# Graph network, two layers in fp32: stores and sums on GpSimd moved, a normalisation's sums given to ScalarE, the last block's weighted sums by quarters

## Chip, cores and metric

The kernel runs on one core of a Trainium2 chip. The metric is the device time of one execution in microseconds. TensorE is called PE in the profile's lines, VectorE DVE, ScalarE ACT, GpSimd POOL and SyncE SP.

## What is computed

128 graphs of 64 nodes with 768 features pass through two residual layers, each followed by a layer normalisation. All is fp32. The reference, cut to what matters:

```
def layer0(h, adjacency):
    u = einsum('bld,bmd->blm', h, h) / sqrt(d)
    delta = softmax(u) * adjacency
    attn = delta / (sum(delta, axis=2, keepdims=True) + 1e-10)
    h_left, h_self, h_right = h @ W_left.T + b_left, h @ W_self.T + b_self, h @ W_right.T + b_right
    ctx = upper(attn) @ h_left + diagonal(attn) * h_self + lower(attn) @ h_right
    o = (ctx - mean(ctx)) / sqrt(var(ctx) + 1e-12) * gamma + beta
    return relu(o)

def layer1(x, adj):                       # 12 heads of 64
    q, k, v = heads(x @ Wq + bq), heads(x @ Wk + bk), heads(x @ Wv + bv)
    s = q @ k.T / sqrt(64) + beta * adj
    s = where(adj > 0, s, -9e15)
    return merge(softmax(s) @ v)

x = layernorm(x + layer0(x, adj))         # eps 1e-5
x = layernorm(x + layer1(x, adj))
```

## The kernel before

The 8192 node rows are worked in 16 blocks (n = 0 to 15) of 512 tokens: four tiles (T = 4) of 128 tokens, two graphs in each. The large products (left, right, self, values, queries and keys) are not done as plain matrix products. `seven` (L343) does a product as seven sub-products of half size (Strassen-Winograd), each for j = 0 and 1. The sums of inputs that this needs are formed on GpSimd: `combined` (L296 to L301) and `combined4` (L307), tiles `S`. For blocks 3 to 15 (`DEEP` = 3) the left and right products together go through a second level, `nested` (L398) called by `both_sides`, with 49 sub-products of matmuls of 128x384; its inputs `q` are quarter sums from GpSimd (L314 to L317), its weights `wlr` come from DRAM (`lr_d`), where `deepened` put differences of weights (L250) during blocks 0 and 1.

A sub-product accumulates in a PSUM bank, X or Y. Between the sub-products that share a bank the partial result is taken out: in `nested` as `u_deep` or `lr` (L414 by ScalarE where nothing is added, L416 by VectorE), in the self and value products as `u`, `o` and `v` (L393, L567, L718, L723), in the query and key products as `uqk` (L748, ScalarE), `q` and `k` (L754 ScalarE, L756 VectorE). The next sub-product of that bank waits for it.

The loop over n (L961 on) emits, for m = n + 1 and p = n - 1: the left and right products of block m, its self product, the values of block n with the first layer's context of block m between them (`context0`, four parts), then queries and keys of block n in three head groups hg = 0, 1, 2 (`projected`). The second layer's small work is put between the sub-products. For each head group there are `scores` (64 small products, then on VectorE two multiplications L782, add L803, maximum L804, subtract L805; on ScalarE 16 exponentials L796; on VectorE two transpositions L800 of the exponentials, `turn`) and `weighted` (64 small products `ps_y` L824, then on VectorE a reciprocal L830 and four multiply-adds L834 for each of four parts). `finish_by_act` normalises the finished block on ScalarE (sums L865, squares L868, root L870, output L862) and stores it from GpSimd (L863). In block n's `context0` the first normalisation takes its statistics on VectorE (`moments`: bn_stats L331, aggregate L332, root on ScalarE L339), then gamma and beta, relu and residual (L654, L657, L660), the second normalisation's moments, and `norm` (L666), which also stores the tile to DRAM as `x1d` from GpSimd (L668). `x1d` is loaded again in transposing order by ScalarE's DMA queue (`squares`, L275) as `sq`.

The order of all instructions on an engine is the order in which the program emits them. Work on VectorE and ScalarE is held in two lists, `urgent` and `lazy`; after each sub-product `step` hands out one item of them (items marked "act" also leave room for one more). `settle(key)` empties a list up to the named work. The dictionaries left, right, own, val and qk[0..2] hang work on a place: in `seven`, place 2k + j is before half j of the k-th sub-product; in `nested`, the 28 places of left (0 to 13) and right (14 to 27) are spread over the 49 sub-products. The places that matter here, all in the loop: scores(p, 2) at left 1, weighted(p, 1) at left 5, weighted(p, 2) at left 13, finish_by_act(p) at right 0, the loads of `sq` from x1d (`begin1`) at left 10 to 13, combined4 of block m at left 0, weighted(n, 0) at qk[2] 5. Behind the last block, the weighted sums come in six halves of 32 products, each followed by its additions, and `finish` twice.

Of the kernel before, what the change touches and what calls it, by code (L numbers as in the profile page):

```python
# [17 lines left out]
P = 128  # L18
# [5 lines left out]
T = 4  # L24
# [27 lines left out]
def gnn_two_layers(ctx: ExitStack, tc, x, adj, wl, bl, ws, bs, wr, br, gamma, beta,  # L52
# [81 lines left out]
    def step(act_free=True, light=False):  # L134
        for queue in (urgent, lazy):
            if not queue:
                continue
            kind = queue[0][2] if len(queue[0]) > 2 else None
            if light and (queue is lazy or kind is None):
                return  # L140
            if kind == "act" and not act_free:
                continue
            queue.popleft()[1]()
            if kind is None or light:
                return
# [252 lines left out]
    def nested(width, sums, load, multiply, view, C, bias0, bias1, hooks):  # L398
# [65 lines left out]
        for k, i in enumerate(ORDER2):  # L464
            after = ORDER2[k + 1] if k + 1 < len(ORDER2) else None
            if after:
                F[after], W[after] = sums(after), load(after)
            for j in (6, 5, 7):
                sub(i, j)
            if after:  # L470
                sub(after, 1)
                sub(after, 2)
            for j in (4, 3):
                sub(i, j)
# [159 lines left out]
    def context0(n):  # L634

        blk = blocks[n]
        xa, o, dg = blk["xa"], blk["x"], blk["dg"]

        def part(t):
# [8 lines left out]
            if t == T - 1:  # L648
                rest()

        key = ("o", n)

        def affine(t, mean, rstd):
            nc.vector.scalar_tensor_tensor(o[t], o[t], mean, affine_of["gamma"], ALU.subtract, ALU.mult)  # L654
# [10 lines left out]
        def norm(t, mean, rstd):  # L665
            nc.vector.tensor_scalar(o[t], o[t], mean, rstd, ALU.subtract, ALU.mult)  # L666
            if squared:
                nc.gpsimd.dma_start(out=x_d[t * P : (t + 1) * P, :], in_=o[t])  # L668

        def rest():  # L670
            for t, mr in enumerate(moments(key, o, 1e-12)):
                later(key, partial(affine, t, *mr), partial(affine2, t, *mr), partial(residual, t))
            for t, mr in enumerate(moments(key, o, 1e-5)):
                later(key, partial(norm, t, *mr))

        return [partial(part, t) for t in range(T)]
# [28 lines left out]
    def values(n, hooks={}, in_place=False):  # L705
# [8 lines left out]
        def last(t, h, ps, part):  # L714
            add = pairs(bias["v"][:, h * HALF : (h + 1) * HALF] if part is None else part)
            heads = slice(h * 3, (h + 1) * 3)
            if not in_place:
                nc.vector.tensor_tensor(v[:, t, :, heads, 0:HD], pairs(ps), add, ALU.add)  # L718
                return
            for r in range(2):  # L720
                for g in range(2):
                    rows = slice(g * L, (g + 1) * L)
                    nc.vector.tensor_tensor(v[r * L : (r + 1) * L, t, g, heads, 0:HD],  # L723
                                            pairs(ps)[rows, r], add[rows, r], ALU.add)

        by_tokens("v", blocks[n]["S"], last, None, hooks)
        if not in_place:
            low, high = v[0:L, :, 1, :, 0:HD], v[L:P, :, 0, :, 0:HD]
            swap = l0t.tile([P, T, HP, HD], F32, tag="lr", name="swap")
            later(("v", n), act(lambda: nc.scalar.copy(swap[0:L], high)), act(lambda: nc.scalar.copy(high, low)),  # L730
                  act(lambda: nc.scalar.copy(low, swap[0:L])), queue=urgent)
# [77 lines left out]
    def weighted(n, hg, halves=range(2)):  # L809
# [7 lines left out]
        for h in halves:  # L817
            for t in range(2):
                for c in range(2):
# [7 lines left out]
        def added(h, r):  # L827
            ps = y[r, h]
            rz = st.tile([P, 2, 2], F32, tag="rz1", name="rz1")
            nc.vector.reciprocal(rz, ps[:, :, :, HD])  # L830
            for t in range(2):
                res = xt[2 * h + t].rearrange("p (c k r d) -> p r c k d", c=2, k=HC, r=2)
                for c in range(2):
                    nc.vector.scalar_tensor_tensor(res[:, r, c, hg, :], ps[:, t, c, 0:HD], rz[:, t, c : c + 1],  # L834
# [5 lines left out]
    def finish_by_act(n):  # L840
# [19 lines left out]
        def norm(ts):  # L860
            for t in ts:
                nc.scalar.activation(xt[t], xt[t], AF.Identity, bias=shift[:, t : t + 1], scale=rstd[:, t : t + 1])  # L862
                nc.gpsimd.dma_start(out=out_t[n, t], in_=xt[t])  # L863
# [7 lines left out]
              act(partial(norm, (0, 1))), act(partial(norm, (2, 3))), queue=urgent)  # L871
# [42 lines left out]
    now(context0(0))  # L914
# [35 lines left out]
    for n in range(NBLK):  # L950
# [12 lines left out]
        for i, (when, hooks, place) in zip(ORDER2, ((0, val, 2), (0, val, 8), (0, qk[0], 8), (0, qk[1], 6),  # L963
                                                    (0, qk[2], 6), (1, left, 2), (1, right, 4))):
# [6 lines left out]
        if p >= 0:  # L971
            one, two, three = (left, left, right) if not last else (qk[0], qk[1], qk[1])
            at(one, 1 if not last else 2, scores, p, 2, 1 if last else 2)
            at(one, 5, weighted, p, 1)
            at(two, 13 if not last else 5, weighted, p, 2)
            at(three, 0 if not last else 6, finish if last else finish_by_act, p)

        if not last:
            if n > 0:
# [9 lines left out]
                at(left, 10, begin1)  # L989
# [8 lines left out]
                for a in range(P // Q):  # L998
                    at(left, 10 + a, lambda a=a: sq1["fs"][a]())
# [14 lines left out]
                at(left, 0, lambda: combined4(blocks[m]["S"]))  # L1014
# [20 lines left out]
            for t, f in enumerate(context0(m)):  # L1035
                at(val, 1 + 2 * t, f)
            if m + 1 < NBLK:
# [25 lines left out]
        if not last:  # L1063
            at(qk[2], 5, weighted, n, 0)
        for hg in range(NHG):
            projected(n, hg, qk[hg])
    n = NBLK - 1
    values(n, {6: [partial(scores, n, 2, 2, l0t)]}, True)

    for h in range(2):  # L1070
        for hg in range(NHG):
            weighted(n, hg, (h,))
            settle(("y", n, hg))
        finish(n, range(2 * h, 2 * h + 2))
        settle(("f", n))
# [31 lines left out]
```

## Time and profile before

| | us |
|---|---|
| three runs | 2980.74, 2976.38, 2977.93 |
| median | 2977.93 |
| the profiled execution | 2979.73 |
| its span | 2978.0 |
| PE busy | 2881.8 |
| VectorE busy | 2062.7 |
| ScalarE busy | 994.4 |
| GpSimd busy | 713.0 |
| block 3's stretch, 627 to 807, PE busy | 177.31 of 180.0 |
| the last 110 us, PE busy | 89.95 |

A busy time is the sum of an engine's instructions; weight loads (PEld) run beside the matmuls. The granted clock is the share of its full rate that TensorE was given in a stretch. Idle time is charged by the profile to what seemed to release the engine.

### The profile page before, as it was taken

How to read it: one execution, taken by the hardware profiler on the slowest of the kernel's cores; microseconds unless marked ns; L12 is line 12 of the kernel's file. 1: busy time of each engine (PE TensorE's matmuls, PEld its weight loads, DVE VectorE, ACT ScalarE, POOL GpSimd, SP SyncE). 2: the span in 40 equal slices, each digit the busy share in tenths (PEclk: the TensorE clock that was granted, in tenths of full speed). 3: DMA queues.
4: the chain of work that ended last, by engine and by line, in shares of the span. 5: the costliest groups of instructions: out<-in, count | busy, mean ns of one | idle time of the engine just before them, and what ended most of it. 6: DMA issues, size and time to landing. Idle time of an engine off the chain costs nothing.

```text
span 2978.0 us, 49826 instructions
## 1 busy us (share of the span) xinstructions
PE 2881.8 (97%) x17578; PEld 1940.8 (65%) x17578; DVE 2062.7 (69%) x4219; ACT 994.4 (33%) x1848; POOL 713.0 (24%) x881
## 2 busy tenths in 40 slices
PE   8899899999999999999999999999999999999997
PEld 5557558576675756758566575766758566585685
DVE  5858767677686766757667676776867667577657
ACT  0102305334243351424425253342433514244242
POOL 3133311405023040321304123050230403213010
PEclk9999999999999999999999999999999999999998
DMA  9678875958669495775957759486694957858442
GB/s 328 204 258 271 243 203 158 277 143 257 180 176 265 138 286 156 203 237 155 269 151 219 225 164 274 138 247 191 184 260 136 286 154 191 246 153 273 130 123 86
DMA packets 440149, 613.17 MB, mean 206 GB/s; under 512 B 53584, under 2 KB 416720, under 8 KB 439904
## 3 DMA queue, kind: packets, MB, share of 16 engines
q1 hardware_dynamic: 361808, 492.79, 55.0%
q10 hardware_dynamic: 60848, 44.05, 8.0%
q0 software_dynamic: 17248, 73.15, 6.6%
q8 instruction: 143, 2.34, 0.3%
q14 instruction: 102, 0.84, 0.1%
HBM read 539.43 MB, written 77.27 MB: 207 GB/s over the span
## 4 chain that ended last, share of the span: by engine, by line
PE 79%; DVE 6%; issue 6%; ACT 5%; DMA 3%; POOL 1%; SPq 0%; ACTq 0%; POOLq 0%; DVEq 0%
PE ps_X L362 32%; PE ps_Y L362 24%; PE ps_Y L613 9%; PE ps_X L613 8%; PE ps_ctx L644 3%; ACT eT L796 3%; PE u L504 1%; PE ps_y L824 1%; PE sc L778 1%; DMA wlr<-lr_d 1%; ACT L796 1%; DVE lr L416 1%; DVE mx L804 1%; DVE s L782 1%; DVE s L805 0%
## 5 line engine op out<-in xcount | busy, mean ns | idle before, releaser
L748 ACT ACTIVATE uqk<-ps_X,bq 128x256 f32<-128x256 f32 x144 | 68.2, 473 | 1056.4 <-PE ps_X L362 909.2
L362 PE MATMUL ps_X<-xT,wqk 128*128 128x256 f32 x1728 | 390.8, 380 | 3.5 <-ACT uqk L748 3.4
L362 PEld LDWEIGHTS ps_X<-xT,wqk 128*128 128x128 f32 x1728 | 329.2, 191 | 52.5 <-ACT uqk L748 4.3
L796 ACT ACTIVATE eT<-s 32x256 f32<-32x256 f32 x768 | 317.8, 414 | 36.8 <-DVE s L805 26.6
L296 POOL TENSOR_TENSOR S<-hT 128x768 f32<-128x768 f32 x16 | 28.9, 1808 | 1157.3 <-PE ps_Y L362 1120.3
L362 PE MATMUL ps_Y<-S,wqk 128*128 128x256 f32 x1152 | 264.3, 379 | 0.0
L362 PEld LDWEIGHTS ps_Y<-S,wqk 128*128 128x128 f32 x1152 | 218.9, 190 | 29.8
L613 PE MATMUL ps_Y<-wlr,q 128*128 128x384 f32 x546 | 208.6, 491 | 0.0
L416 DVE TENSOR_TENSOR lr<-ps_Y,u_deep 128x384 f32<-128x384 f32 x273 | 151.5, 555 | 75.1 <-PE ps_Y L613 66.9
L362 PE MATMUL ps_X<-wv,xT 128*128 128x384 f32 x576 | 195.3, 489 | 0.1
L362 PE MATMUL ps_X<-ws,hT 128*128 128x384 f32 x540 | 181.7, 490 | 4.3 <-DVE u L393 3.0
L613 PE MATMUL ps_X<-wlr,q 128*128 128x384 f32 x364 | 150.1, 494 | 23.9 <-POOL q L314 17.0
L834 DVE SCALAR_TENSOR_TENSOR o<-ps_y,rz,o 128x64 f32<-128x64 f32 x768 | 165.1, 278 | 6.8
L362 PEld LDWEIGHTS ps_X<-wv,xT 128*128 128x128 f32 x576 | 108.1, 190 | 81.3 <-issue 9.0
L362 PEld LDWEIGHTS ps_X<-ws,hT 128*128 128x128 f32 x540 | 103.0, 192 | 77.8 <-DVE u L393 3.6
L416 DVE TENSOR_TENSOR u_deep<-ps_X,lr 128x384 f32<-128x384 f32 x195 | 107.8, 553 | 60.4 <-PE ps_X L613 54.7
L756 DVE TENSOR_TENSOR q<-ps_Y,uqk 128x256 f32<-128x256 f32 x144 | 60.3, 419 | 124.3 <-ACT uqk L748 73.1
L613 PEld LDWEIGHTS ps_Y<-wlr,q 128*128 128x128 f32 x546 | 101.6, 190 | 67.2
L393 DVE TENSOR_TENSOR u<-ps_X,bv 128x384 f32<-128x384 f32 x96 | 52.8, 550 | 128.8 <-PE ps_X L362 128.7
L362 PE MATMUL ps_X<-S,wqk 128*128 128x256 f32 x576 | 138.3, 385 | 0.0
L296 POOL TENSOR_TENSOR S<-xT 128x768 f32<-128x768 f32 x16 | 28.9, 1806 | 452.3 <-DVE xT L284 323.8
L362 PE MATMUL ps_Y<-xT,wqk 128*128 128x256 f32 x576 | 135.6, 385 | 0.0
(238 smaller groups left out, 5441.2 us busy)
## 6 DMA issues: line engine op xcount, KB each, us to landing
wlr<-lr_d SPq DMA_DIRECT2D x819, 192.0 KB, 3.7
wqk<-qk_d SPq DMA_DIRECT2D x672, 192.0 KB, 2.4
wv<-d_v SPq DMA_DIRECT2D x192, 192.0 KB, 2.9
ws<-d_s SPq DMA_DIRECT2D x180, 192.0 KB, 5.3
wv<-in_L_gnn_Wv_dram SPq DMA_DIRECT2D x144, 192.0 KB, 4.1
ws<-in_L_gnn_W_self_dram SPq DMA_DIRECT2D x135, 192.0 KB, 5.5
xa<-in_x_dram SPq DMA_DIRECT2D x64, 384.0 KB, 6.4
out_dram<-o POOLq DMA_DIRECT2D x64, 384.0 KB, 6.6
```

The lines of the kernel that those rows point to most:

```text
L296: nc.gpsimd.tensor_tensor(s1, a21, a22, ALU.add)
L362: nc.tensor.matmul(ps, lhsT=a, rhs=b, start=(c == 0 and i in (1, 2, 5)), stop=(c == len(fs) - 1), skip_group_check=True)
L393: nc.vector.tensor_tensor(u, ps, bias[nm][:, b * HALF : (b + 1) * HALF], ALU.add)
L416: nc.vector.tensor_tensor(dst, view(ps), add, ALU.add)
L504: nc.tensor.matmul(u[g * L : (g + 1) * L, t, :], lhsT=xT[:, c, tok], rhs=xT[:, c, tok], start=(c == 0), stop=(c == KC - 1))
L613: nc.tensor.matmul(ps, lhsT=a, rhs=b, start=(k == 0 and j in (1, 2, 5)), stop=(k == len(fs) - 1), skip_group_check=True)
L644: nc.tensor.matmul(ps[g * L : (g + 1) * L, 0:HALF], lhsT=blk["aT"][:, t, g * L : (g + 1) * L], rhs=blk["lr"][t][:, g, cols], start=True, s ...
L748: nc.scalar.activation(u, ps, AF.Identity, bias=bias["qk"[j]][:, c : c + 1])
L756: nc.vector.tensor_tensor(dst, ps, part, ALU.add)
L778: nc.tensor.matmul(sc[r][g * L : (g + 1) * L, t, c, :], lhsT=q[rows, c, tok], rhs=k[rows, c, tok], start=True, stop=True)
L796: nc.scalar.activation(e[cols, :, rows], pairs[rows, :, cols], AF.Exp)
L834: nc.vector.scalar_tensor_tensor(res[:, r, c, hg, :], ps[:, t, c, 0:HD], rz[:, t, c : c + 1], res[:, r, c, hg, :], ALU.mult, ALU.add)
```

## The change

It has nine parts. `step` runs items marked "free" at the head of a list without using up its step. The stores of x1d and of the output are split off from the normalisations as such free items. The last group of a second-level product does sub-product 3 before 4. `context0` of blocks after the first takes its sums on ScalarE: one Identity with accumulation after each part, four squares at val 9 (`squares`), the root at val 13 (`roots`), reciprocal and the rest at qk[0] 1 (`inverse`). In the last block v is written in one operation for each half, ScalarE then exchanges its halves by three copies for each quarter, and the weighted sums run by quarters (a half of the tiles, a half of the heads), seven of twelve between the value products. Two of the weight matrices of `deepened` (i = 4, 3) move from left 2 and right 4 of block 1 to own 3 and val 3. scores(p, 2) moves from left 1 to 2; weighted(p, 2) from left 13 to right 1 and finish_by_act from right 0 to 2 where m >= DEEP. The loads of sq from x1d start at right 2 in block 1 alone. combined4 of block m moves from left 0 to left 6, weighted(n, 0) from qk[2] 5 to 11.

```
@@ step
         for queue in (urgent, lazy):
+            while queue and queue[0][2:] == ("free",):
+                queue.popleft()[1]()
@@ nested
-            for j in (4, 3):
+            for j in (4, 3) if after else (3, 4):
@@ context0
+        by_act = n > 0
...
-            if t == T - 1:
-                rest()
+            if by_act:
+                nc.scalar.activation(unused(), o[t], AF.Identity, accum_out=total[:, t : t + 1])
+            elif t == T - 1:
+                rest(moments(key, o, 1e-12))
+        def squares():
+            nc.vector.tensor_scalar(nm, total, -1.0 / D, None, ALU.mult)
+            for t in range(T):
+                nc.scalar.activation(unused(), o[t], AF.Square, bias=nm[:, t : t + 1], accum_out=var[:, t : t + 1])
+
+        def roots():
+            nc.vector.tensor_scalar(std, var, 1.0 / D, 1e-12, ALU.mult, ALU.add)
+            nc.scalar.activation(std, std, AF.Sqrt)
+
+        def inverse():
+            nc.vector.reciprocal(rstd, std)
+            rest([(nm[:, t : t + 1], rstd[:, t : t + 1]) for t in range(T)])
...
             for t, mr in enumerate(moments(key, o, 1e-5)):
                 later(key, partial(norm, t, *mr))
+                if t > 0:
+                    later(key, (partial(stored, t - 1), "free"))
+            later(key, GAP, (partial(stored, T - 1), "free"))
@@ values
-    def values(n, hooks={}, in_place=False):
+    def values(n, hooks={}, by_quarters=False):
...
-            for r in range(2):
-                for g in range(2):
-                    rows = slice(g * L, (g + 1) * L)
-                    nc.vector.tensor_tensor(v[r * L : (r + 1) * L, t, g, heads, 0:HD],
-                                            pairs(ps)[rows, r], add[rows, r], ALU.add)
+            nc.vector.tensor_tensor(v[:, t, :, heads, 0:HD], pairs(ps), add, ALU.add)
+            if by_quarters and t % 2:
+                tiles = slice(t - 1, t + 1)
+                swaps(v[0:L, tiles, 1, heads, 0:HD], v[L:P, tiles, 0, heads, 0:HD], swap[0:L, tiles, heads])
+
+        def swaps(low, high, buffer, call=lambda f: f()):
+            for a, b in ((buffer, high), (high, low), (low, buffer)):
+                call(partial(nc.scalar.copy, a, b))
@@ weighted
-    def weighted(n, hg, halves=range(2)):
+    def weighted(n, hg, halves=range(2), heads=range(2)):
...
-                for c in range(2):
+                for c in heads:
@@ finish_by_act
-              act(partial(norm, (0, 1))), act(partial(norm, (2, 3))), queue=urgent)
+              act(partial(norm, (0, 1))), act(partial(norm, (2, 3))), (partial(stored, (0, 1)), "free"),
+              GAP, GAP, (partial(stored, (2, 3)), "free"), queue=urgent)
@@ the loop
-                                                    (0, qk[2], 6), (1, left, 2), (1, right, 4))):
+                                                    (0, qk[2], 6), (1, own, 3), (1, val, 3))):
...
-            at(one, 1 if not last else 2, scores, p, 2, 1 if last else 2)
+            at(one, 2, scores, p, 2, 1 if last else 2)
             at(one, 5, weighted, p, 1)
-            at(two, 13 if not last else 5, weighted, p, 2)
-            at(three, 0 if not last else 6, finish if last else finish_by_act, p)
+            if not last and m < DEEP:
+                at(left, 13, weighted, p, 2)
+                at(right, 0, finish_by_act, p)
+            else:
+                at(three, 1 if not last else 5, weighted, p, 2)
+                at(three, 2 if not last else 6, finish if last else finish_by_act, p)
...
-                at(left, 10, begin1)
+                when, place = (left, 10) if n > 1 else (right, 2)
+                at(when, place, begin1)
...
-                at(left, 0, lambda: combined4(blocks[m]["S"]))
+                at(left, 6, lambda: combined4(blocks[m]["S"]))
...
+            for hooks, place, f in ((val, 9, normal[0]), (val, 13, normal[1]), (qk[0], 1, normal[2])):
+                at(hooks, place, f)
...
-            at(qk[2], 5, weighted, n, 0)
+            at(qk[2], 11, weighted, n, 0)
@@ after the loop
-    values(n, {6: [partial(scores, n, 2, 2, l0t)]}, True)
+    hooks = {2: [partial(scores, n, 2, 2, l0t)]}
...
-    for h in range(2):
-        for hg in range(NHG):
-            weighted(n, hg, (h,))
-            settle(("y", n, hg))
-        finish(n, range(2 * h, 2 * h + 2))
-        settle(("f", n))
+    def quarter(m, h, hg):
+        weighted(n, hg, (m,), (h,))
+        settle(("y", n, hg))
+
+    for place, *which in ((6, 0, 0, 0), (7, 0, 0, 1), (11, 0, 0, 2), (11, 1, 1, 0), (12, 1, 1, 1), (12, 1, 1, 2),
+                          (13, 1, 0, 0)):
+        hooks.setdefault(place, []).append(partial(quarter, *which))
+    values(n, hooks, True)
+    quarter(1, 0, 1)
+    quarter(1, 0, 2)
+    finish(n, (2, 3))
+    step()
+    step()
+    for hg in range(NHG):
+        weighted(n, hg, (0,), (1,))
+        settle(("y", n, hg))
+    finish(n, (0, 1))
+    settle(("f", n))
```

## The prediction

> **What bounds the kernel now.** I read the page first, then the granted clock by stretches, then the timeline of TensorE at each place the change touches.
>
> The page's rows of busy time, clock and chain:
>
> ```profile
> PE 2881.8 (97%) x17578; PEld 1940.8 (65%) x17578; DVE 2062.7 (69%) x4219; ACT 994.4 (33%) x1848; POOL 713.0 (24%) x881
> ...
> PEclk9999999999999999999999999999999999999998
> ...
> PE 79%; DVE 6%; issue 6%; ACT 5%; DMA 3%; POOL 1%; SPq 0%; ACTq 0%; POOLq 0%; DVEq 0%
> ```
>
> TensorE works 2881.8 of 2978.0 us; all its idle time is 96 us, and no engine's sum matters but TensorE's waits. In a steady block (180.1 us from a place to the same place a block later, three blocks alike in the timeline) it idles under 3 us. A part of this change is worth only the TensorE wait it removes or makes, times the blocks that have it.
>
> The largest wait (timeline; columns start, length, engine, line, operation, and in brackets idle time and its supposed releaser) is at block 1's left product:
>
> ```profile
> 342.04 2.92 ACTq L275 DMA_DIRECT2D sq<-x1d  x3
> ...
> 345.00 1.28 ACT L796 ACT_TABLE_LOAD   x1 [18.09 <-issue]
> 346.29 3.40 ACT L796 ACTIVATE eT<-s 32x256 f32<-32x256 f32 x8
> ...
> 350.58 2.01 PE L824 MATMUL ps_y<-v,eT 64*64 64x65 f32 x64 [13.76 <-DVE eT L800]
> ...
> 352.52 3.80 PE L362 MATMUL ps_Y<-wl,S 128*128 128x384 f32 x6
> ```
>
> ScalarE's queue first issues the loads of x1d (L275), which wait for GpSimd's stores of it (L668), and only then the exponentials. TensorE loses 13.76 us. After it the clock is low (columns: stretch, busy time by engine, granted clock, DMA):
>
> ```profile
> 24.00:28.00 4.00, 3.04 (x5) 1.85 (x6) 3.86 (x11) 0.00 (x0) 0.71 (x2) 0.59 1.06 405
> ...
> 140.00:147.00 7.00, 3.97 (x9) 2.32 (x9) 6.71 (x15) 0.00 (x0) 0.00 (x0) 0.80 1.07 339
> ...
> 350.00:352.00 2.00, 1.42 (x52) 1.45 (x56) 1.02 (x2) 0.00 (x0) 0.00 (x0) 0.50 1.07 335
> 352.00:356.00 4.00, 4.00 (x30) 2.41 (x23) 0.00 (x0) 0.00 (x0) 0.00 (x0) 0.53 1.12 247
> 356.00:360.00 4.00, 4.00 (x13) 2.30 (x13) 3.53 (x13) 0.25 (x1) 0.00 (x0) 1.00 1.14 178
> ...
> 2856.00:2862.00 6.00, 4.05 (x24) 3.76 (x24) 1.30 (x2) 5.03 (x13) 1.31 (x1) 1.00 0.06 21
> ```
>
> At 0.5, 64 products that elsewhere take 1.16 us took 2.01, and six that take 2.10 took 3.80: 2.5 us more. A gap of 2.47 us at 24.96 and one of 3.03 at 143 each cost about 3.4 us at half rate ((1-0.59)x4/0.5 = 3.3; (1-0.80)x7/0.5 = 2.8 and a remainder in the next stretch); one of 1.95 us at 2858 cost none.
>
> The start of a second-level product, in a block that stands for thirteen:
>
> ```profile
> 687.12 3.39 ACT L796 ACTIVATE eT<-s 32x256 f32<-32x256 f32 x8
> ...
> 690.53 0.48 ACT L414 COPY u_deep<-ps_X 128x384 f32<-128x384 f32 x1
> ...
> 691.11 0.88 PE L613 MATMUL ps_X<-wlr,q 128*128 128x384 f32 x2 [1.43 <-POOL q L314]
> ...
> 697.70 6.81 ACT L796 ACTIVATE eT<-s 32x256 f32<-32x256 f32 x16
> ...
> 708.07 0.56 DVE L416 TENSOR_TENSOR u_deep<-ps_X,lr 128x384 f32<-128x384 f32 x1
> ...
> 709.05 0.81 PE L613 MATMUL ps_X<-wlr,q 128*128 128x384 f32 x2
> ```
>
> The wait of 1.43 us is charged to GpSimd's L314. That ended at 690.77; the copy L414, which empties the PSUM bank that the product writes, ended at 691.01, 0.1 us before the start, and stood in ScalarE's queue behind eight exponentials. I take the copy.
>
> **Per second-level block (13 of them).** Start-to-start losses, wait included, against a pitch of 0.323 us a product.
>
> Left start, removed. hg 0's weighted sums move from place 5 to 11, so the last exponentials of hg 1 are given out earlier, and in the changed program no exponential stands before that copy; combined4 (1.82 us, L307) leaves GpSimd's queue there too, so under either releaser 1.58 us goes, and 0.41 us at the scores' wait for k (687.15): -1.98.
>
> Left, a later subtraction. Scores of hg 2 come one sub-product later. Add, max and subtract (L803-805, pitch 1.14 us) move behind the weighted sums: VectorE's lr (707.42, 0.46 pitch), then the subtraction (1.14), then u_deep, ending 709.58 instead of 708.63. TensorE's next X (709.05) starts at 709.63: +0.58.
>
> Left, a transposition that waits. The sixteen exponentials (6.81 us, row above) now run 709.17-715.98 instead of 697.7-704.5. VectorE's queue has the first transposition, then two lr, the second transposition, and u_deep: 716.0 + 0.63 + 2x0.55 + 0.63 + 0.56 = 718.9. TensorE wants that u_deep at 717.17 (718.37 less the 1.2 us of weighted sums that now come after it): +1.67. What is late next is hg 2's weighted sums and the finish: VectorE's o is due about 9 us later than before, the four stores then start near 742 and land at 6.6 us (page) by 751; the self product's first write, at 750.3 before, comes at 752.5. That cover is 1 us and it costs nothing while it holds. The x1d loads now stand between the two halves of the exponentials: waiting for stores issued over 10 us earlier, I charge 0 (0.3 us each, the row of the one at 349.83, if not).
>
> Sub-products (3,4) instead of (4,3), last group. Three now needs both u_deep and the lr behind it on VectorE (0.56 us each), where four needed the first only: +0.59.
>
> Query/key stage of hg 1. ScalarE now takes the first normalisation's sums (4 at 0.84 + 0.19, 4 squares at 0.94 + 0.19: +8.5 us), VectorE loses 8 bn_stats (0.534) and 4 aggregates (0.208): -5.1. The products of v (28 us) run over it, so I cost the move at nothing; without that cover an evacuation would wait behind one square, 1.13. But x1 is ready earlier, so the square root of the second normalisation moves forward, from after the stage to between two groups of exponentials:
>
> ```profile
> 840.88 1.69 ACT L796 ACTIVATE eT<-s 32x256 f32<-32x256 f32 x4
> ...
> 842.59 0.47 ACT L754 ACTIVATE q<-ps_X,bq 128x256 f32<-128x256 f32 x1
> ...
> 843.09 1.69 ACT L796 ACTIVATE eT<-s 32x256 f32<-32x256 f32 x4
> ...
> 844.80 0.47 ACT L754 ACTIVATE k<-ps_X,bk 128x256 f32<-128x256 f32 x1
> ...
> 848.58 1.28 ACT L339 ACT_TABLE_LOAD   x1
> ```
>
> Now: exponentials to 842.57, table load 1.28, root 0.20, q 0.47, table load 1.28, exponentials 1.69, k 0.47: 848.05. TensorE's last X there needs k's bank and was due at 846.60: +1.45. The Trainium skill ("ScalarE: Activation LUTs", What ACT_TABLE_LOAD costs) gives a switch of set 1.28 us of load and 1.38 of drain. No drain shows here: the load at 848.58 follows uqk's end (848.56) and the root starts 849.87. By the page this wait would be 2.76 us longer in each block; I go by the row.
>
> Sum: -1.98 + 0.58 + 1.67 + 0.59 + 1.45 = +2.31; with 0.1 for the changes of bank and tile, 2.4 a block, +31 in thirteen. Ends: 1.3 if the four waits are each 0.27 shorter because VectorE comes free sooner, 3.0 with two x1d loads at 0.3. Splitting the stores from the normalisations leaves their number (8 issues of 0.55 to 0.59) and GpSimd, idle for 76% of the span, covers them: nothing; uncovered, x1d's loads come up to 2.3 later, and their transpositions first run in the self product.
>
> **Blocks 0 and 1.** The same root stands before a uqk in block 0's hg 2 stage (uqk at 303.9 instead of 301.13, bank due at 302.4): +2.0; block 1's hg 1 stage: +1.45. Block 1's left: the exponentials of hg 2 now come before the x1d loads (moved to the right product), so -13.76 and -2.5. But both transpositions stand behind the two lr of the Y product that ends at 336.82, themselves behind lr, a normalisation (0.63) and aT (0.69): 338.35 + 0.65 = 339.0, a new gap of 2.2 us. It lies between the gap that cost no clock (1.95) and the one that did (2.47): 0 to 1.7, I take 0.8. Together 2.0 + 1.45 - 16.26 + 3.0 = -9.8. The weight differences of two matrices (16 subtractions of 0.58, 8 stores) move from left and right to self and values of block 1, where the timeline shows VectorE idle for over 10 us together: nothing, and up to the 9.3 us of its time if that idle time is elsewhere.
>
> **Last block.** Without quarters VectorE takes 8 x 1.46 us for v; with them 8 x 0.56, and ScalarE 12 copies of about 0.5 (0.48 for 128x384, 0.83 for 64x768). But the first quarter needs v behind this VectorE queue: exponentials of hg 1 end 2933.30 as before, two transpositions 1.30, two multiplications 1.25, v 0.56: 2936.4; add 1.14, second v, and three copies: 2939.6. TensorE was free at 2933.5: 6.1 us waited, against 0 before, and about 1.7 us of clock. Seven quarters of 16 products take 2.8 us there, 0.8 is waited at the second copy, 0.3 at joints: the last large product ends 11.7 us later. After it VectorE has v (0.76), five quarters at 1.2 (half of the row pattern of a reciprocal and four L834 in 0.98, twice), statistics of two tiles twice (2.6 each, from 2958.73), 1.4 for the first normalisation, 0.5 for the last root, and from the last normalisation 6.0 as before (2971.98 to 2978.0): 19.9 instead of 28.4. Net +3.2; ends -3 (no clock loss, half the wait) and +8 (low clock to the end, as from 2955 on before).
>
> **The sum.** 31 - 9.8 + 3.2 = +24.4 on a profiled run of 2979.73 (span 2978.0 and 1.7 around it), 0.06% over the median of 2977.93: 3002.
>
> **Rivals.** (A) The left product's new waits do not bind: VectorE's order is hidden, since it has lost 5.1 us of work a block. For: 69% busy. Against: the waits are for ScalarE's exponentials, which begin later, not for VectorE's load. 13 x (0.58 + 1.67 + 0.59) = 37 less: 2965, faster. It decides once the exponentials end 1.7 us earlier, by 714.3. (B) The early root finds no place before q and k, because its deviation is ready later than 842.6: 15 places, 22 us less: 2980. Against: statistics of VectorE can end by 841.4 there. (C) The x1d loads still hold block 1: 3002 + 13.8 + 2.5 - 3.0 = 3015. Against: no exponential follows them in ScalarE's order.
>
> **How the numbers follow.** My forecast has 0.62 (its own range 2988 to 3014: 13 blocks by -1.1 and +0.6, with the tail's +5 above), A 0.14, B 0.14, C 0.10. No change is 0.2%, 6 us, about what the measurement can tell. A is faster; B lies two thirds slower-or-same: faster 0.16, same 0.08, slower 0.76. From 2975 to 3014, A and part of C are left out, 0.2.
>
> **What would show it.** Block period near 182.5 us; at the left start no gap of 1.43; about 1.7 us of TensorE idle behind a u_deep that follows a transposition; a table load between two groups of exponentials in hg 1's stage with 1.5 us idle after; no 13.76 us gap; 2.9 and 3.2 us gaps at the first quarter. Wrong if the block period stays at or below 180.1.

## The result and the profile after

The changed kernel took 3000.52 us (median of four runs, 2997.80 to 3001.49) beside 2977.15 (median of four, 2975.95 to 2980.74): a ratio of 1.0075, 95% interval 1.0058 to 1.0092. It is slower by 23 us; 3002 was forecast. The profiled execution took 3000.49, its span 2998.8, 20.8 over the 2978.0 of before. Line numbers have moved: exponentials L827, their transposition L831, subtraction L836, second-level products L615 and their evacuations L418 (VectorE) and L416 (ScalarE), `uqk` L779, q and k L785, `ps_y` L855, v L747, roots L341, loads of `sq` L277, stores of x1d L695.

The page after, the same three rows (busy time, clock, chain):

```profile
PE 2887.6 (96%) x17578; PEld 1936.3 (65%) x17578; DVE 1979.1 (66%) x4042; ACT 1117.4 (37%) x2100; POOL 720.9 (24%) x881
...
PEclk9999999999999999999999999999999999999998
...
PE 84%; issue 5%; ACT 4%; DMA 2%; DVE 2%; POOL 2%; SPq 0%; ACTq 0%; POOLq 0%; DVEq 0%
```

VectorE lost 84 us of work, ScalarE took on 123, and the kernel is slower. TensorE's idle time went from 96 to 111 us and its busy time is 5.8 us more for the same 17578 matmuls. So the page names no engine; the places do. I laid the two traces beside each other by TensorE's own landmarks (the first product of each stage):

| from landmark to landmark | forecast, us | measured, us |
|---|---|---|
| start to block 0's values | 0 | +2.4 |
| block 0's values, queries and keys | +2.0 | +6.5 |
| block 1's left product | -13.3 | -13.5 |
| thirteen block periods, and block 1's hg 1 stage | +32.5 | +27.1 |
| last block's transposition, queries and keys | 0 | -4.6 |
| last block's values to the end | +3.2 | +2.9 |
| sum | +24.4 | +20.8 |

The steady block (period by the starts of the value products) went from 180.13 to 182.57, +2.44 each; thirteen make 31.7. Three of before's periods were longer, by 2.4, 0.4 and 1.9, for waits on loads that after didn't have: hence 27.1.

A left product in the steady part, the same place that the prediction showed for before (timeline: start, length, engine, line, operation, idle time before it and its supposed releaser):

```profile
706.71 1.69 ACT L827 ACTIVATE eT<-s 32x256 f32<-32x256 f32 x4 [11.81 <-DVE s L836]
...
707.24 0.88 PE L615 MATMUL ps_X<-wlr,q 128*128 128x384 f32 x2 [0.81 <-issue]
...
708.28 0.32 ACTq L277 DMA_DIRECT2D sq<-x1d  x1
...
708.41 5.12 ACT L827 ACTIVATE eT<-s 32x256 f32<-32x256 f32 x12
...
713.56 0.71 DVE L831 STREAM_TRANSPOSE eT<-eT 128x512 f32<-128x512 f32 x1 [2.47 <-ACT eT L827]
...
715.72 0.52 DVE L418 TENSOR_TENSOR u_deep<-ps_X,lr 128x384 f32<-128x384 f32 x1
...
716.34 0.88 PE L615 MATMUL ps_X<-wlr,q 128*128 128x384 f32 x2 [1.32 <-issue]
```

The wait of 1.43 at the product's start is gone. Two new ones stand for it: 0.81 us behind a `u_deep` that follows the subtraction (0.81 in this block alone, whose period is 182.91; 0.45 or 0.46 in the other twelve second-level blocks), and 1.32 us behind a `u_deep` that follows two transpositions, which follow the last of sixteen exponentials (ending 713.53). "issue" names no releaser; the evacuation of the bank ended 0.10 us before both starts (707.14, 716.24). The load of `sq` between the exponentials takes nothing: the exponentials go on 0.01 us after the four before it.

The third wait in that product stands in its last group, where sub-product 3 now comes first (same view; the kernel before waits 0.65 there, for the `u_deep` of sub-product 4):

```profile
741.80 1.53 PE L615 MATMUL ps_Y<-wlr,q 128*128 128x384 f32 x4 [1.29 <-issue]
```

The hg 1 stage of queries and keys, same view:

```profile
843.17 1.28 ACT L341 ACT_TABLE_LOAD   x1
...
844.46 0.20 ACT L341 ACTIVATE std<-std 128x4 f32<-128x4 f32 x1
844.58 0.46 ACT L785 ACTIVATE q<-ps_X,bq 128x256 f32<-128x256 f32 x1
...
845.05 1.28 ACT L827 ACT_TABLE_LOAD   x1
...
846.34 1.69 ACT L827 ACTIVATE eT<-s 32x256 f32<-32x256 f32 x4
848.05 0.47 ACT L785 ACTIVATE k<-ps_X,bk 128x256 f32<-128x256 f32 x1
...
848.58 0.70 PE L364 MATMUL ps_X<-xT,wqk 128*128 128x256 f32 x2 [1.24 <-ACT k L785]
```

The root has come between two groups of exponentials with a table load on either side; k, which empties the bank, is late and TensorE waits 1.24.

Block 0's hg 2 stage (same view), where only 2.0 us had been charged:

```profile
303.30 1.28 ACT L827 ACT_TABLE_LOAD   x1
...
304.59 1.70 ACT L827 ACTIVATE eT<-s 32x256 f32<-32x256 f32 x4
306.31 0.47 ACT L779 ACTIVATE uqk<-ps_X,bq 128x256 f32<-128x256 f32 x1
...
306.84 1.22 PE L364 MATMUL ps_X<-xT,wqk 128*128 128x256 f32 x2 [3.58 <-ACT uqk L779]
```

Block 1's left product, where before lost 13.76 us (same view):

```profile
345.22 1.12 DVE L587 TENSOR_TENSOR lr<-ps_Y,u 64x384 f32<-64x384 f32 x2
346.38 1.30 DVE L831 STREAM_TRANSPOSE eT<-eT 128x512 f32<-128x512 f32 x2
347.24 2.02 PE L855 MATMUL ps_y<-v,eT 64*64 64x65 f32 x64 [2.61 <-DVE eT L831]
```

The loads of `sq` no longer stand ahead; the transpositions come behind the additions to `lr` on VectorE, and 2.61 us are left.

And the clock behind the large waits (stretch, length, then busy time and instructions of PE, PEld, DVE, ACT and POOL, granted clock, DMA share, GB/s):

```profile
140.00:150.00 10.00, 6.97 (x22) 3.84 (x21) 10.00 (x24) 1.28 (x1) 0.00 (x0) 1.00 1.04 321
300.00:312.00 12.00, 8.43 (x87) 6.56 (x86) 5.16 (x18) 7.40 (x14) 8.20 (x7) 0.76 0.47 143
344.00:350.00 6.00, 3.39 (x68) 2.38 (x68) 3.61 (x7) 0.00 (x0) 0.29 (x1) 0.76 0.83 302
2844.00:2850.00 6.00, 4.02 (x19) 3.23 (x18) 2.38 (x6) 5.88 (x12) 0.00 (x0) 1.00 0.37 100
2956.00:2960.00 4.00, 2.59 (x17) 1.69 (x18) 3.93 (x10) 2.77 (x7) 0.00 (x0) 0.50 0.00 0
```

0.76 over 12 us means 2.9 us of lost clock behind the 3.58 us wait: together the 6.5 of the table.

Last, the first quarter of the last block (timeline):

```profile
2951.19 1.30 DVE L831 STREAM_TRANSPOSE eT<-eT 128x512 f32<-128x512 f32 x2 [6.86 <-ACT eT L827]
2952.42 1.25 DVE L813 TENSOR_TENSOR s<-sc,m 128x512 f32<-128x512 f32 x2
2953.59 0.54 DVE L747 TENSOR_TENSOR v<-ps_Y,u 128x384 f32<-128x384 f32 x1
...
2954.19 0.33 PE L855 MATMUL ps_y<-v,eT 64*64 64x65 f32 x2 [2.55 <-DVE v L747]
...
2957.41 0.71 PE L855 MATMUL ps_y<-v,eT 64*64 64x65 f32 x14 [2.89 <-ACT v L752]
```

TensorE waits for v behind VectorE's queue, then for the three copies on ScalarE.

### The profile page after: what moved, and what is told of

Its sections match the earlier page's. It is cut to its first block, busy times and chain, and to the rows that moved or that the text cites. A ratio compares the mean times of both kernels' runs of the same rounds, so it can differ in the third digit from the quotient of the medians.

```text
span 2998.8 us, 49953 instructions
## 1 busy us (share of the span) xinstructions
PE 2887.6 (96%) x17578; PEld 1936.3 (65%) x17578; DVE 1979.1 (66%) x4042; ACT 1117.4 (37%) x2100; POOL 720.9 (24%) x881
## 4 chain that ended last, share of the span: by engine, by line
PE 84%; issue 5%; ACT 4%; DMA 2%; DVE 2%; POOL 2%; SPq 0%; ACTq 0%; POOLq 0%; DVEq 0%
PE ps_X L364 32%; PE ps_Y L364 24%; PE ps_Y L615 11%; PE ps_X L615 10%; PE ps_ctx L653 3%; PE ps_y L855 2%; PE sc L809 2%; ACT eT L827 2%; PE u L506 1%; POOL q L317 1%; ACT L341 1%; ACT L827 1%; DMA b_k<-in_L_gnn_Wk_dram 0%; POOL q L316 0%; POOL q L318 0%
## 5 line engine op out<-in xcount | busy, mean ns | idle before, releaser
L364 PE MATMUL ps_X<-xT,wqk 128*128 128x256 f32 x1728 | 398.8, 382 | 21.6 <-ACT k L785 16.1
L827 ACT ACTIVATE eT<-s 32x256 f32<-32x256 f32 x768 | 317.8, 414 | 181.3 <-DVE s L836 171.5
L695 POOL DMA_DIRECT2D x1d<-o x56 | 30.8, 550 | 1085.8 <-DVE o L691 1077.7
L658 ACT ACTIVATE unused<-o 128x768 f32<-128x768 f32 x60 | 50.6, 843 | 514.4 <-DVE o L655 354.8
L615 PE MATMUL ps_Y<-wlr,q 128*128 128x384 f32 x546 | 209.5, 493 | 16.8 <-issue 16.8
L418 DVE TENSOR_TENSOR lr<-ps_Y,u_deep 128x384 f32<-128x384 f32 x273 | 151.7, 556 | 92.8 <-PE ps_Y L615 80.7
L779 ACT ACTIVATE uqk<-ps_X,bq 128x256 f32<-128x256 f32 x144 | 68.0, 472 | 328.3 <-PE ps_X L364 326.6
L615 PE MATMUL ps_X<-wlr,q 128*128 128x384 f32 x364 | 152.3, 500 | 28.9 <-issue 23.0
L615 PEld LDWEIGHTS ps_Y<-wlr,q 128*128 128x128 f32 x546 | 100.5, 190 | 88.2 <-issue 24.4
L418 DVE TENSOR_TENSOR u_deep<-ps_X,lr 128x384 f32<-128x384 f32 x195 | 107.1, 549 | 68.1 <-PE ps_X L615 67.6
L364 PE MATMUL ps_Y<-wv,S 128*128 128x384 f32 x384 | 135.7, 496 | 0.0
```

The costliest lines, as they stand in the source:

```text
L364: nc.tensor.matmul(ps, lhsT=a, rhs=b, start=(c == 0 and i in (1, 2, 5)), stop=(c == len(fs) - 1), skip_group_check=True)
L418: nc.vector.tensor_tensor(dst, view(ps), add, ALU.add)
L615: nc.tensor.matmul(ps, lhsT=a, rhs=b, start=(k == 0 and j in (1, 2, 5)), stop=(k == len(fs) - 1), skip_group_check=True)
L658: nc.scalar.activation(unused(), o[t], AF.Identity, accum_out=total[:, t : t + 1])
L779: nc.scalar.activation(u, ps, AF.Identity, bias=bias["qk"[j]][:, c : c + 1])
L827: nc.scalar.activation(e[cols, :, rows], pairs[rows, :, cols], AF.Exp)
```

## The experiments

All but the last are single runs; kernels of one set ran on one chip, with a run of the kernel before beside them (2974.77 for the first set of four, 2980.14 for the second, 2980.47, median of seven, for the third), so whole times of different sets compare to about 5 us. The block period repeats to 0.1 us in most blocks of a trace (182.56 or 182.57 in eleven of the changed kernel's thirteen), and is what I read. My theory: the steady block is slower for ScalarE's order and VectorE's queue (late exponentials, early root, sub-product 3 before 4). Its rivals: GpSimd's tiles, the loads of `sq`, or the sums given to ScalarE.

**First set: one edit each.** `four_before_three`, the changed kernel with the last group's order put back:

```
-            for j in (4, 3) if after else (3, 4):
+            for j in (4, 3):
```

> The changed kernel with sub-products 4, 3 in the last group as before. My theory: the 1.29 us gap (ps_Y of sub-product 3) becomes the 0.65 us gap of before (ps_X of 4): 0.64 us in 13 blocks, span 2990.5. Rival (the wait is for GpSimd's quarter sums or the later finish, whatever the order): a gap of 1.2 us or more remains at that place and the span stays within 3 us of 2999.

Span 2989.6: 9.2 less than after. The wait at the group's start is 0.65 instead of 1.29, the period 181.96 instead of 182.57. Confirmed: 0.61 a block, 7.9 in thirteen. The rest of the 9.2 lies outside the blocks that the edit touches: between block 0's and block 1's values this execution is 2.7 shorter, since the low clock behind the same waits of 3.58 and 2.61 us was shorter or absent (0.86 over 304 to 316, 1.00 over 345 to 353), and it starts 1.0 later.

`scores_one_earlier`, hg 2's scores back at left 1:

```
-            at(one, 2, scores, p, 2, 1 if last else 2)
+            at(one, 1 if not last else 2, scores, p, 2, 1 if last else 2)
```

> The changed kernel with scores(p, 2) at left 1 instead of 2. My theory: the subtraction comes before the additions of hg 1's weighted sums again, the exponentials start some 11 us earlier, so the 0.81 us gap goes back to 0.21 and the 1.32 us gap behind the transposition goes to about 0.2; the scores wait for k again (0.2 to 0.4): 13 x (0.6 + 1.1 - 0.3) = 18 less, span 2981. Rival (VectorE's and ScalarE's load in the left product makes the waits, and the weighted sums moved into the right product): both gaps stay above 0.6 us and the span within 5 us of 2999.

Span 2968.0, 30.8 less; I had expected 18 less. Both waits are gone (the largest there is 0.21 us), and the wait for k did not come back. The period is 180.31: 2.26 a block, which is what the prediction charged to the two (0.58 + 1.67 = 2.25). My later expectation had been too careful, the prediction's terms were right. This one line of the change costs 13 x 2.26 = 29 us, more than the whole loss.

`root_later`, the changed kernel with the second half of the first normalisation later, so that the root misses the exponentials of hg 1:

```
-            for hooks, place, f in ((val, 9, normal[0]), (val, 13, normal[1]), (qk[0], 1, normal[2])):
+            for hooks, place, f in ((val, 9, normal[0]), (val, 13, normal[1]), (qk[0], 5, normal[2])):
```

> The changed kernel with `inverse` at qk[0] 5 instead of 1, nothing else: ScalarE still takes the first normalisation's sums, but the root of the second one is given out four steps later, behind k's evacuation of hg 1's stage. If the place of the root between two groups of exponentials makes the wait (my theory): the 1.24 us gap of 14 blocks goes (1.5 us each with its start), and the 3.58 us gap of block 0 with its half clock (6.5 us): span 2998.8 - 21 - 6.5 = 2971. If ScalarE's added work makes it (rival): the gaps stay within 0.3 us and the span within 5 us of 2999.

Span 3034.6, a miss by 64 us. The 1.24 and 3.58 us waits are gone, as the theory says. But x1 is stored later, and the loads of `sq` in ScalarE's queue wait for that (timeline of the left product):

```profile
703.34 3.41 ACT L827 ACTIVATE eT<-s 32x256 f32<-32x256 f32 x8 [11.82 <-DVE s L836]
...
704.25 0.56 POOL L695 DMA_DIRECT2D x1d<-o  x1
...
707.33 0.32 ACTq L277 DMA_DIRECT2D sq<-x1d  x1
707.69 3.40 ACT L827 ACTIVATE eT<-s 32x256 f32<-32x256 f32 x8 [0.94 <-DMA x1d<-o]
...
711.12 0.71 DVE L831 STREAM_TRANSPOSE eT<-eT 128x512 f32<-128x512 f32 x1 [3.39 <-ACT eT L827]
...
713.90 0.88 PE L615 MATMUL ps_X<-wlr,q 128*128 128x384 f32 x2 [2.25 <-issue]
```

The second eight exponentials wait 0.94 for a store issued 3 us earlier, and the wait behind the transposition grows from 1.32 to 2.25, in the other twelve blocks to 3.40 to 3.88, with a low clock behind it in all but one (0.74 over 712 to 718; full clock behind the 3.41 at 1457.01). The period is 184 to 187. So the early root is not all loss: it bought the early store that makes the loads of `sq` free in the changed kernel. The two edits are coupled through ScalarE's queue.

`before_combined4_later`: which releaser holds the left start of before, the quarter sum on GpSimd that the profile names or the copy on ScalarE? The kernel before, with combined4 alone moved:

```
-                at(left, 0, lambda: combined4(blocks[m]["S"]))
+                at(left, 6, lambda: combined4(blocks[m]["S"]))
```

> The kernel of before with combined4 of block m at left 6 instead of 0, nothing else. The profile charges the 1.43 us gap at the left start to GpSimd's quarter sum behind combined4. My theory (the copy on ScalarE behind eight exponentials): the gap stays at 1.4 us in all 13 blocks, span within 3 us of 2978. Rival (GpSimd's queue): the gap goes below 0.3 us, 13 x 1.2 = 16 us less, span 2962.

Span 2978.6 and period 180.13 in most blocks, both as before; the wait is there (timeline):

```profile
691.22 0.45 POOL L315 TENSOR_TENSOR q<-q,hT 128x128 f32<-128x128 f32 x1
...
692.67 0.48 ACT L414 COPY u_deep<-ps_X 128x384 f32<-128x384 f32 x1
...
693.25 0.88 PE L613 MATMUL ps_X<-wlr,q 128*128 128x384 f32 x2 [1.42 <-POOL q L317]
```

The first quarter sums are done by 691.67 now, 1.6 us before the start, and TensorE still starts 0.10 after the copy. GpSimd alone was not it; the name in brackets has moved to another GpSimd line, and is as wrong. In the kernel before, though, the two were close. The sum that this product reads is that of L315, and there it is on record until 691.31, the product from 691.11 (the profile's times of GpSimd are rough):

```profile
690.85 0.46 POOL L315 TENSOR_TENSOR q<-q,hT 128x128 f32<-128x128 f32 x1
```

So this run shows that the copy holds the product by itself; it doesn't show that GpSimd would not have held it had the copy come earlier.

**Second set: parts together.** `root_later_scores_earlier`, the changed kernel with the edits of `four_before_three`, `scores_one_earlier` and `root_later` at once. ("The run before" in its text is `sums_on_vector`, which stands next here.)

> As the run before, but the sums stay on ScalarE and `inverse` stands at qk[0] 5. If root_later lost its gain only because x1d's later stores held the second half of the exponentials of hg 2, which with scores at left 1 start 11 us earlier: the 1.24 and 3.58 us gaps are gone, and at most 0.3 us a block remains behind the transposition, span 2935. If the stores still hold the last exponentials: a gap of 1.5 us or more behind the transposition in each block, span above 2960.

Span 2944.9, expected 2935. The 1.24, 3.58 and 1.32 us waits are all gone, the loads of `sq` no longer bind; the period is 179.07. What is left over what I expected is a new wait of 0.60 at a `uqk` in each block, since the weighted sums, which stood before that product at qk[2] 5, are now at 11.

`sums_on_vector`, the sums and squares put back on VectorE as well:

```
-        by_act = n > 0
+        by_act = False
...
-            for hooks, place, f in ((val, 9, normal[0]), (val, 13, normal[1]), (qk[0], 1, normal[2])):
-                at(hooks, place, f)
```

with scores at left 1 and 4 before 3 (root later has no meaning there).

> The changed kernel with scores(p, 2) at left 1, sub-products 4, 3 as before, and context0's first statistics on VectorE as before (bn_stats; no ScalarE sums). From the runs so far the first two give 2968.0 - 9.2 = 2958.8. My theory: with the statistics on VectorE the second root falls behind hg 1's stage again: the 1.24 us gap goes from 14 blocks (1.5 each) and block 0's 3.58 us gap with its half clock (6.5): span 2931. Rival (the sums on ScalarE pay by freeing VectorE of 5.1 us a block): new TensorE gaps behind VectorE in the value or query stages, span 2945 or more.

Span 2951.9, expected 2931 (rival 2945 or more). The period is 179.06, the same as with the sums on ScalarE. So giving the sums to ScalarE is worth nothing in a steady block, though it frees VectorE of 5 us. The span lies where the rival put it, but not for gaps in the steady blocks: the 1.24 and 3.58 us waits are gone, and the same 0.60 for a `uqk` stands in each block as in the run above. The 7 us between the two spans lie in single waits, 3.10 in the first second-level block (542.37, for a `u_deep` on VectorE, with a low clock behind it: that period is 6.1 longer) and 3.40 in the last block's queries and keys.

`sq_loads_at_left`, the loads of `sq` in block 1 back at left 10, to see what made the 13.76 us of before:

```
-                when, place = (left, 10) if n > 1 else (right, 2)
+                when, place = left, 10
```

> The changed kernel with x1d's loads at left 10 in block 1 too, as in all other blocks and as before. My theory (the place of the loads in ScalarE's queue alone made the 13.76 us gap): the loads stand between the exponentials of hg 2 again and wait for the stores: the 2.61 us gap grows to 9 us or more, with half clock, span 3008 or more. Rival (earlier normalisation and the weight differences moved to self and values took the gap away): it stays below 4 us, span within 3 us of 2999.

Span 3001.5, expected 3008 or more (rival: wait under 4); what came lies between the two. Timeline:

```profile
345.64 0.32 ACTq L277 DMA_DIRECT2D sq<-x1d  x1
346.01 1.69 ACT L827 ACTIVATE eT<-s 32x256 f32<-32x256 f32 x4 [14.70 <-DMA x1d<-o]
...
350.30 2.01 PE L855 MATMUL ps_y<-v,eT 64*64 64x65 f32 x64 [8.10 <-DVE eT L831]
```

The exponentials wait for the store again, and TensorE 8.10 us instead of 2.61. The place of the loads is 5.5 of the 11.2 us between 13.76 and 2.61. The other half came with the rest of the change; whether by the stores off the normalisations, the sums on ScalarE or the weight differences moved out of that product was not tried apart.

`quarters_later`, the last block's scores at value place 6 and five quarters between the products, from place 9, the rest behind:

```
-    hooks = {2: [partial(scores, n, 2, 2, l0t)]}
+    hooks = {6: [partial(scores, n, 2, 2, l0t)]}
...
+    for place, *which in ((9, 0, 0, 0), (10, 0, 0, 1), (12, 1, 1, 0), (12, 1, 1, 1), (13, 1, 0, 0)):
...
```

> The changed kernel with the last block's scores of hg 2 at place 6 of the values as before, and quarters (0,0,0), (0,0,1), (1,1,0), (1,1,1), (1,0,0) at places 9, 10, 12, 12, 13, the other seven behind. My theory (the early scores put VectorE's copies of v behind transpositions that wait for ScalarE): the gaps of 2.55 and 2.89 us go, five quarters hide under products: from the first value product to the end 52 to 54 us instead of 60.2, span 2992. Rival (ScalarE's copies of v behind the exponentials hold the quarters wherever they stand): gaps of 3 us or more in sum before y in the value stage, and no less than 58 us.

From the first value product to the end 61.4 us, against 60.2 for the change and 57.3 before; I had expected 52 to 54, so a miss, and the rival's case. The 2.55 and 2.89 us waits are gone, but sixteen exponentials got ahead of the second exchange of v (timeline):

```profile
2963.02 6.79 ACT L827 ACTIVATE eT<-s 32x256 f32<-32x256 f32 x16
...
2969.84 0.51 ACT L752 COPY swap<-v 64x384 f32<-64x384 f32 x1
...
2971.48 0.80 PE L855 MATMUL ps_y<-v,eT 64*64 64x65 f32 x14 [5.17 <-ACT v L752]
```

The wait moved and stayed at 5.2 us. The copies need ScalarE at a time when it holds 6.8 us of exponentials.

**Third set: the part that pays.** `before_weighted_later`, the kernel before with a single line of the change:

```
-            at(qk[2], 5, weighted, n, 0)
+            at(qk[2], 11, weighted, n, 0)
```

> The kernel of before with weighted(n, 0) at qk[2] 11 instead of 5, nothing else. If the copy behind eight exponentials makes the 1.43 us gap, this alone removes it, since the exponentials are then given out before that copy: gap gone in 13 blocks and with it the scores' wait for k, 13 x 2.0 = 26 us less, span 2952. If GpSimd's combined4 and quarter sums make it, the gap stays at 1.2 us or more, span within 5 us of 2978.

Span 2955.5, against 2952 expected, 22.5 less than before's: 15.9 from the thirteen periods, 4.7 because before's profile has waits for loads that this one hasn't, and the rest outside the steady blocks. Timeline at the left start:

```profile
685.98 0.48 ACT L414 COPY u_deep<-ps_X 128x384 f32<-128x384 f32 x1 [2.68 <-PE ps_X L613]
...
688.36 0.81 PE L613 MATMUL ps_X<-wlr,q 128*128 128x384 f32 x2
```

The copy runs at once, and the product follows without a wait: the other half of the case for the copy. (GpSimd's L315, which ends at 688.34, came earlier too, by 2.2 us against the start of the left product, so this run alone would not tell the two apart; `before_combined4_later` shows that the copy is enough to make the wait.) The period is 178.91, 1.22 under before: 1.98 gained, 0.76 given back at the 0.60 us wait for `uqk`.

`parts_that_pay` keeps of the change the split stores, the sums on ScalarE, the moved weight differences, loads and combined4, and weighted(p, 2) and finish_by_act at right 1 and 2; scores go to left 1, 4 stays before 3, `inverse` goes to qk[0] 5, weighted(n, 0) to qk[2] 10, and the last block is that of before.

> The changed kernel with scores(p, 2) at left 1, sub-products 4, 3 as before, `inverse` at qk[0] 5, weighted(n, 0) at qk[2] 10 and the last block's values and weighted sums as before. root_later_scores_earlier had 2944.9; weighted sums at place 10 fill the 0.60 us gap before a uqk bank (0.76 with its start, 14 blocks: -10), the old tail is worth 60.7 - 57.3 = 3.4: span 2931, time 2933. If the gap is not the late bank but ScalarE's load, it stays and the span is 2941.

2936.31 us, median of four runs (2933.09 to 2936.77) beside 2980.47: a ratio of 0.9854, 95% interval 0.9838 to 0.9871. Busy times of its page:

```profile
PE 2870.7 (98%) x17578; PEld 1936.8 (66%) x17578; DVE 1983.0 (68%) x4054; ACT 1113.9 (38%) x2088; POOL 713.3 (24%) x881
```

The span of the profiled run is 2931.3, as expected; it is the fastest of the four, and the median lies 3 us over the 2933 that I had written. In nine of the thirteen blocks the period is 178.2 to 178.4 with one wait over 0.55 us left, the 0.65 between sub-products 4 and 3. In the other four it is 179.3 to 180.2: a `u_deep` on VectorE stands behind the finish's mean (L881), which waits for ScalarE's sums, which come behind a load of `sq`, and TensorE waits 1.07 to 2.04 (the first at 1070.26). Why the load comes later in these four was not settled. Place 10 instead of 11 took the `uqk` wait away. The kernel beats both others; 23.9 of the 46.7 us less than before come from the thirteen periods, 15.1 from the stretch between block 0's and block 1's values.

## Why the prediction was right, and where it was off

Slower was right, and the mechanism too. By its steps:

- **Left start.** -1.98 forecast; the wait is gone. That the copy makes it is shown by moving the GpSimd work (no change) and by moving the exponentials out of the copy's way (wait gone). The prediction's reason against GpSimd was weaker than it looked: it read the end of L314, where the product needs L315, which was as late as the copy. Its term holds under either releaser, as it said.
- **Later subtraction and late transposition.** +0.58 and +1.67 forecast (the last by its own figures, 718.9 less 717.17, is 1.73). With the scores moved back both vanish, 2.26 together. Rival A, that VectorE's lighter load would hide them, falls: it needed exponentials ending some 2.9 us before TensorE wants the bank. In the block shown TensorE wanted it at 714.85, 1.49 before it started, and they ended at 713.53, only 1.3 before.
- **3 before 4.** +0.59 forecast, 0.61 measured.
- **Root between the exponentials.** +1.45 forecast; between starts the product loses 1.40. Each table load took 1.28 us and nothing more: it starts 0.01 us behind q, and exponentials start 0.01 us behind it. The 1.38 us of drain that the Trainium skill gives ("ScalarE: Activation LUTs", What ACT_TABLE_LOAD costs) do not appear; by my estimate the wait would have been some 4 us with it. Rival B, no early root, falls. What the prediction did not see is that the root's earliness pays elsewhere (`root_later`).
- **The sums on ScalarE cost nothing.** Shown: equal periods of 179.07 and 179.06 either way. In the last block they gain, which the prediction had not counted (below).
- **Loads of `sq` between exponentials, charged 0.** Right for the changed kernel, with little cover: stores a few microseconds later make it 0.94 and more.
- **The self product's first write.** It was to come within 1 us of its cover's end; no wait stood there, as forecast.
- **Block 1's left.** -13.3 forecast, -13.5 measured; the new wait is 2.61 where 2.2 was worked out, and the clock was low behind it (0.76 over 344 to 350). Rival C falls with it.
- **Last block.** +3.2 forecast, +2.9 measured. The waits were 5.44 instead of 6.1, the clock took 2.9 instead of 1.7 (0.50 over 4 us, 0.78 over the next 4), and from the last large product to the end it was 19.5 instead of 19.9.

**The term that was mis-sized** is block 0's root, +2.0 forecast, +6.5 measured. The prediction took the bank as due at 302.4, as before. But weighted(n, 0) had moved from before that product to qk[2] 11, and without its products the bank was due at 300.7 (306.84 less 3.74, less the 2.4 by which this trace runs later); `uqk` ended on that scale at 304.4, just as worked out. The wait came to 3.58, 3.74 between starts, and behind it lay a low clock, 2.9 us, that the sum did not have. The clock was chance (the last section shows on what it hangs): in `scores_one_earlier` the same wait of 3.58 had full clock behind it (1.00 over 306 to 312), and the stretch grew by 3.6 instead of 6.5. The prediction subtracted the moved weighted sums in the left product and forgot them here.

**Outside the sum**: before waits 3.40 us for a `uqk` (at 2826.61; twelve products behind it took 4.54 us) in the last block's queries and keys, after only 1.98 (at 2847.64), and the 1.95 of before at 2857.99 is gone: -4.6 that I had not looked for. The runs say which part did it: all four kernels with the first normalisation's sums on VectorE (before, `before_combined4_later`, `before_weighted_later`, `sums_on_vector`) have that wait at 3.40 or 3.41, and none of those with the sums on ScalarE has it; with the `inverse` at qk[0] 5 it is under 0.7. The +2.4 at the start (a wait of 2.05 at 169.43 and a low clock behind it) and the 4.7 us of waits for loads in the profile of before come from executions, as far as the runs tell: kernels with the same code up to there begin block 0's values anywhere between 210.9 and 215.4. What makes a start late was not settled. Without these two, the forecast of 24.4 would have stood against 20.8 - 2.4 + 4.7 = 23.1. That the whole came so close is in part luck: +4.5 at block 0's root and -4.6 in the last block's queries and keys, neither foreseen, cancel. The steady blocks, +2.4 forecast and +2.44 measured, are not luck: each of their terms was found at its place.

## What to carry to other kernels

Where an engine empties the banks that TensorE needs, its order is the schedule: for each move, write down what stands ahead of the next evacuation in that queue, in every stage and not only in the one that the move is meant for. A releaser named by a profile is a candidate, and two can end within tenths of a start; moving one alone shows cheaply whether it holds. Taking 5 us a block off VectorE gained nothing in a steady block; moving one line out of a copy's way gained 1.2 us a block, 16 in thirteen.

## What the runs showed of the hardware

A low clock followed waits of 2.05 (0.58 over 169 to 173 in the changed kernel), 2.25 (`root_later`), 2.55 with 2.89, 2.61 and 3.58 us. But length alone does not decide. A wait of 3.03 us at 143 brought a low clock in the kernel before (0.80 over 140 to 147), and the same wait of 3.03, at 143.90, none in the changed one (1.00 over 140 to 150). A wait of 3.58 brought none in `scores_one_earlier` (1.00 over 306 to 312), and one of 2.61 none in `four_before_three` (1.00 over 345 to 353). A wait of 1.95 brought none in the kernel before (1.00 over 2856 to 2862), and the same wait a low one in `before_combined4_later` (0.72 over 2856 to 2862).

The granted clock in the traces tells more. Apart from the ends of a trace, a low stretch lasts 3.41 us or a whole number of times that, and within one trace all of them start whole steps of 3.41 us apart: in the changed kernel one from 306.19 to 313.02 and one from 347.15 to 350.56, twelve steps on. What the cases differ in is how idle TensorE was in the step before. It was busy for 0.49 us of the step that ended at 306.19 and for 0.89 of the one that ended at 347.15; in `scores_one_earlier` the same wait of 3.58 us was split by the end of a step (busy 1.49 us from 302.79 to 306.20 and 1.76 from 306.20 to 309.62), and the clock stayed at 1.00. In the twelve traces every step at full clock with an idle share over 0.6 had a low one behind it; from 0.54 to 0.6 it went either way, and below that a low one came only behind the small products of the weighted sums.

The Trainium skill ("TensorE: Matmul & The Clock Gate", What's actually happening) lets the clock fall to half after at least one idle window of about 3.4 us, with windows that run freely. The half, the window's length and its free running agree with these rows; that the window be idle throughout doesn't, since an idle share of 0.6 was enough.
